# A two-layer scan convolution on one core: output stores over two DMA queues, later statistics, another order in the first sweep

## The chip, the cores and the metric

The kernel runs on one core of a Trainium2 chip. A core has five engines with an instruction stream each: TensorE (PE in the profile) multiplies matrices, VectorE (DVE) and ScalarE (ACT) work on rows of elements, GpSimd (POOL) does so too, and SyncE (SP) only starts transfers. Transfers between the on-chip memory and the DRAM are started by an instruction on SP or on ScalarE, each with a queue of its own (SPq and ACTq in the profile), and are carried out by 16 DMA engines that both queues share. The metric is the device time of one execution in microseconds (us), median of three runs.

## The reference

The input is x with 32 batches, 48 channels, 64 rows and 128 columns, in 32-bit floats. Each of two layers computes `x = x + conv(gn(x))`: gn normalizes each batch over 16 groups of 3 channels, and conv is four recurrent sweeps over the picture, each of the form

```python
def step(w, b):
    def f(carry, inp):
        nxt = inp + _conv1d(carry, w, b)
        return (nxt, nxt)
    return f
...
_, d_rest = jax.lax.scan(step(down_w, down_b), d0, xs[1:])
...
_, u_rest = jax.lax.scan(step(down_w, down_b), u0, seq)
...
_, r_rest = jax.lax.scan(step(right_w, right_b), r0, ws[1:])
...
_, l_rest = jax.lax.scan(step(left_w, left_b), l0, R[Ww - 2::-1])
```

The convolution has 5 taps along the row (or column) and mixes all 48 channels. First the rows are swept downwards and upwards, 63 steps each, then the columns to the right and to the left, 127 steps each. A step needs the one before it, so a sweep is a chain; different batches are independent.

## The kernel before

**Groups and phases.** The 32 batches are cut into four groups of 8. The list `PHASES` fixes an order of twelve phases: eight row phases, each with one layer and one group, sweep down and then up (2 x 63 steps); four column phases, each with one layer and a pair of groups, sweep right and then left (2 x 127 steps). In the profile a sweep has a name such as step_00d: layer, group or pair, direction. Phases are counted from 0 here; phases 2, 6, 10 and 11 are the column phases, and 10 and 11 make the output of the second layer.

**A step.** `step` (L629) issues nine products of 128x128 (L640), which the profile shows as 18 matmuls, into three PSUM tiles; VectorE adds bias and input to each tile and writes the new row or column back in place (L649). The next step's matmuls read that.

**Memory.** The picture of a phase lies in three slots of `arena`; four more pieces, `stage`, hold tiles in passing. Rows and columns need different layouts. The change of layout goes through the DRAM: `move_rows` (L500) stores finished rows or loads rows, in pieces by E8 = 8 rows; `load_unit` (L544) loads one of the six units of a quarter (j = 0 to 3, 32 columns each) for a column phase. A quarter that doesn't fit is spilled and fetched again (`spill_unit`, L559). All transfers are started in one helper, so the profile shows them at L182; without a queue argument they go to SP.

**First group.** Before the first sweep nothing can overlap, so `first_group` (L911) writes out its order by hand. It loads the input in two parts (L945: rows 0 to 31 and 32 to 63, two rows of the picture side by side), takes statistics, permutes each row into the layout of the kernel (`permute`, L473, four copies at L482 per row), stores it (`put_out`), loads it back in the right partitions (`move_rows`), and scales it with the statistics: `scale_rows` (L517) by 24 activations on ScalarE (L525), `scale_at_once` (L529) by two operations on VectorE or GpSimd (L536). The permuted rows of the second part pass through a ring of three places, `more`, in weight tiles that aren't filled yet; row r takes place r mod 3.

**Other groups and the agenda.** Everything beside the sweeps is put on a list, `agenda`, with a due time counted in steps (`at`, L719). Before each step, all entries that have come due are issued (`catch_up`, L1043), and `in_order` (L186) ties every instruction behind the last one of the same engine. So a due time fixes the place of the work in the instruction stream of its engine, and an engine takes its stream in order. `plan_input` (L732) enters the reading of groups 1 to 3: chunks are loaded, permuted on GpSimd and measured by ScalarE (`take_others`, L331: sums at L347, squares at L339). After the last chunk `scaling` (L245) is entered through `spread`, one piece a step: short operations on VectorE, TensorE and ScalarE that turn the sums into scale and offset.

**Seams.** Where a column phase follows directly on the row phase of the same pair (phases 1 and 2, phases 5 and 6), `plan_rows` (L754) stores the last rows in smaller pieces, in `cuts`, and `plan_cols` (L789) loads the first quarter's matching pieces over ScalarE's queue.

**Output of the second layer.** For each unit of phases 10 and 11, in the order of the quarters 3, 2, 1, 0 and in each quarter six units, `load_residual` (L572) loads the layer's input into one of two tiles, over ScalarE's queue (6 or 8 transfers); `add_permuted` (L605) adds it to the result in eight operations on GpSimd (L614), permuting, into one of two tiles; `store_result` (L618) stores it to `out` (12 or 16 transfers, 96, 64 or 32 KB, in runs of 128 bytes), over SP's queue. The unit after next waits for both tiles. On SP's queue the loads of phase 11 stand among these stores. The last quarter of phase 11 goes another way (`last_loads`, `last_results`, L864): its residuals are loaded into free space, VectorE adds (L871), and ScalarE, GpSimd and VectorE share 48 permuting copies (L879) before `store_result`.

Of the kernel before, what the change touches and what calls it, by code (L numbers as in the profile page):

```python
# [35 lines left out]
P = ODD + C  # L36
# [5 lines left out]
GB = 8  # L42
E8 = 8
# [48 lines left out]
def kernel(  # L92
# [8 lines left out]
    nc = tc.nc  # L101
    B, _, H, W = x.shape
# [78 lines left out]
    def dma(dst, src, queue=None):  # L181
        (queue or nc.sync).dma_start(dst, src)  # L182
# [435 lines left out]
    def store_result(k, j, i, perm):  # L618
        pair = PHASES[k][2]
        o, r = divmod(i, 2)  # L620
        both = out[2 * pair * GB : 2 * (pair + 1) * GB]
        dst = both.rearrange("b c (a e) w -> e a c b w", e=E8)[..., j * WQ : (j + 1) * WQ]
        src = perm.rearrange("p (a b n) -> p a b n", a=HH, b=2 * GB)
        for a in range(HH):
            for e, c0, c1, p0 in pieces(o):
                dma(dst[e, r * HH + a, c0:c1], src[p0 : p0 + c1 - c0, a])


    def step(key, weights, b_at, src, inp, dst, whole, part):  # L629
# [89 lines left out]
    def at(t, fn, *args):  # L719
        agenda.append((t, len(agenda), fn, args))  # L720

    def spread(t, gen, every):


        def go(t):
            if next(gen, "end") != "end":
                at(t + every, go, t + every)
                agenda.sort(key=lambda a: a[:2])

        at(t, go, t)  # L730

    def plan_input(g, times, work, lag, nats, perms):  # L732

        stats = InputStats(f"x{g}", GB // 2 if g == 1 else 0)
        rows = nats[0].shape[-1] // W
        ahead, pieces_of = len(nats), rows * W // BN
        per = rows * W * GB // perms[0].shape[-1]
        for j, t in enumerate(times):
            nat = nats[j % ahead]
            if j == 0 and g > 1:  # L740
                at(t - 7, take_in, g, 0, nat)
            for i in range(per):
                perm, r = perms[i % len(perms)], i * rows // per
                at(t + i * work / per, permute, nat, r, perm, [nc.gpsimd])
                at(t + i * work / per + 4, put_out, g, 2 * rows * j + r, perm, rows)
            for b in range(stats.nv):
                at(t + lag + 1.25 * b, stats.take, pieces_of * j, nat, b)
            at(t + lag, stats.take_others, pieces_of * j, nat)
            if j + ahead < len(times):
                free = t + max(work, lag + 1.25 * stats.nv, 7)  # L750
                at(free, take_in, g, 2 * rows * (j + ahead), nat)
        spread(t + work + lag, scaling(f"x{g}", 0, g, stats, x_masks), 1)

    def plan_rows(k, t0, prev):  # L754
        if k == 1:
            ahead, scaled = (-34, -18, 2, 18), (-14, -2, 17, 33)
        elif prev == "cols":
            ahead, scaled = (-28, -12, 4, 20), (-13, 3, 19, 35)
        else:
            ahead, scaled = (-54, -43, 0, 11), (-22, -8, 16, 30)  # L760
        if k:
            for i in range(4):
                at(t0 + ahead[i], move_rows, k, i * LOAD, (i + 1) * LOAD, False)
                at(t0 + scaled[i], scale_rows, k, i * LOAD, (i + 1) * LOAD)

        cuts = list(range(0, H + 1, E8))
        following = PHASES[k + 1][0] == "cols"
        if following and follows(k + 1):
            cuts = [0, E8 // 2] + cuts[1:]
        for h0, h1 in zip(cuts, cuts[1:]):  # L770
            t = t0 + 2 * (H - 1) - h0
            if k == 0:
                t += 24 if h0 >= HALF else 40
            elif not following:
                t = t0 + 92 + 5 * (H - h1) / E8 + (34 if h1 <= HALF else 0)
            at(t, move_rows, k, h0, h1, True)
        at(
            t0 + H - 1,
            nc.gpsimd.tensor_copy,
            last.rearrange("p (o n) -> p o n", o=NG),  # L780
            row(k, H - 1),
        )
# [6 lines left out]
    def plan_cols(k, t0, prev):  # L789
        _, layer, pair = PHASES[k]  # L790
        n = 2 * NG
        after = prev == "cols"
        for i in range(n):
            if follows(k) and UNITS[i][1] == 1:
                other = nc.scalar
                at(t0 - 13 + i, load_unit, k, 0, i, 2, NH, 0, E8, other)
                at(t0 - 6 + i / n, load_unit, k, 0, i, 1, 2, 0, E8, other)
                at(t0 - 3, load_unit, k, 0, i, 0, 1, E8 // 2, E8, other)
                at(t0, load_unit, k, 0, i, 0, 1, 0, E8 // 2, other)
                at(t0 + 1.5, load_unit, k, 1, i)  # L800
            else:
                early = 30 if after else 46 if k == 2 else 70
                at(t0 - early + 2 * i, load_unit, k, 0, i)
                at(t0 + (3 if after else 0.5 if follows(k) else -24 + 2 * i), load_unit, k, 1, i)
            at(t0 + (38 if after else 8) + 2 * i, load_unit, k, 2, i)
            at(t0 + 33 + 2 * i, spill_unit, k, i, False)
            at(t0 + 50 + 2 * i, load_unit, k, 3, i)
        final = k == len(PHASES) - 1
        left = t0 + W - 1
        end = left + W - 1  # L810
        for i in range(n):
            at(left + 64 + 2 * i, spill_unit, k, i, True)
        units = []
        for n_done, j in enumerate((3, 2, 1, 0)):
            every = 4.5
            if j == 0 and PHASES[k + 1 if not final else k][0] == "rows":
                every = 7
            units += [(left + 34 + 32 * n_done + every * i, j, i) for i in range(n)]
        stats = None
        if layer == 0:  # L820
            stats = ResultStatsV(f"r{2 * pair}"), ResultStatsA(f"r{2 * pair + 1}")
        tiles = [stage[:, i] for i in range(4)]
        nats, perms = (tiles, None) if layer == 0 else (tiles[0:2], tiles[2:4])
        ahead = len(nats)

        for u, (t, j, i) in enumerate(units):
            nat = nats[u % ahead]
            o, half = UNITS[i]
            if u < ahead:
                at(left + 16, load_residual, k, j, i, nat)  # L830
            elif not (final and j == 0):
                at(units[u - ahead][0] + (3 if layer == 0 else 5), load_residual, k, j, i, nat)
            if layer == 0:
                at(t, add_residual, k, j, i, nat)
                at(t + 4, keep_result, k, j, i)
                unit = quarter(k, j)[:, half, o]
                if half == 0:
                    for b in range(GB):
                        at(t + 5 + b, stats[0].take, j, o, unit, b)
                else:  # L840
                    at(t + 1, stats[1].take, j, o, unit)
            elif not (final and j == 0):
                perm = perms[u % 2]
                at(t, add_permuted, k, j, i, nat, perm, [nc.gpsimd])
                at(t + 5, store_result, k, j, i, perm)
        if layer == 0:
            t = units[-1][0] + 14
            g = 2 * pair
            spread(t, scaling(f"r{g}", 1, g, stats[0], r_masks), 1)
            spread(t + 20, scaling(f"r{g + 1}", 1, g + 1, stats[1], r_masks), 1)  # L850
        if final:
            at(left + 97, last_loads, k)
            at(end + 4, last_results, k)
# [57 lines left out]
    def first_group():  # L911
# [38 lines left out]
        perms = [spare["down1"][0:P, 0 : W * GB]]  # L950
        perms += [row_views(0)[0][0:P, o, 24:32].rearrange("p h n -> p (h n)") for o in range(NG)]
        more = [spare[k][0:P, 0 : W * GB] for k in ("down1", "right", "left")]

        def permute_row(i, r, *engines):
            permute(parts[i], r, (more if i else perms)[r % (3 if i else 4)], engines)

        def put_row(i, r):
            put_out(0, i * HALF + r, (more if i else perms)[r % (3 if i else 4)], rows)

        def rows_by_product(h0, n):  # L960
            src = parts[0][0:C].rearrange("p b (r k e) -> p e r k b", k=NK, e=E8)
# [50 lines left out]
        for _ in scaling("x0", 0, 0, stats, x_masks):  # L1012
            pass
        scale_at_once(0, 0, 4, nc.vector)
        scale_at_once(0, 4, 8, nc.gpsimd)
        for r in range(2, 8):
            permute_row(0, r, nc.scalar if r % 2 else nc.gpsimd)
            put_row(0, r)
        scale_rows(0, 8, 16)
        for r in range(3):  # L1020
            permute_row(1, r, nc.gpsimd)
            put_row(1, r)
        move_rows(0, 16, 32, False)
        scale_rows(0, 16, 24)
        for r in range(3, 16):
            permute_row(1, r, *([nc.gpsimd] if r < 12 else [nc.gpsimd, nc.scalar]))
            put_row(1, r)
        scale_rows(0, 24, 32)
        move_rows(0, 32, 48, False)
# [77 lines left out]
```

## Time and profile before

| What | us |
|---|---|
| median of three runs (4600.73 to 4604.13) | 4602.15 |
| the profiled execution, first to last instruction | 4604.0 |
| first matmul of step_00d starts | 109.9 |
| last matmul of step_00d starts | 288.8 |
| step_00r (phase 2), first and last matmul start | 712.0, 987.8 |
| step_10l (phase 10), first and last matmul start | 3589.5, 3844.7 |
| step_11r (phase 11), first and last matmul start | 3855.5, 4234.0 |
| step_11l, first and last matmul start | 4234.3, 4489.6 |

The granted clock of TensorE over the span is 0.959. The profile's list of waits names an engine and line, what ended the wait, and three numbers: us in total, how often, and the longest. A wait that needed several things is put down to the one that came last. The chain of waits is followed backwards from the last instruction: each piece is what the next one waited for. The windows give, for each stretch, the busy time of each engine and the share of time in which the 16 DMA engines had a packet in work; the share is a sum over packets and can exceed 1 a little where packets of two queues overlap. Of the stores to `out`, 384 have 96 KB and take 2.6 us from issue to landing (median); the issue of a store itself takes 0.52 us of SP (median).

### The profile page before, as it was taken

What the parts mean: (1) busy time and instruction counts of PE and PEld (TensorE: products, weight loads), DVE (VectorE), ACT (ScalarE), POOL (GpSimd) and SP (SyncE); (2) the same over time, 40 slices, a digit from 0 to 9 for tenths busy, and PEclk for the clock granted to TensorE, in tenths of its full rate; (3) what the DMA queues carried; (4) which work ended last, traced back from release to release, by engine and by line L of the source; (5) the groups of instructions that cost most, each with busy time, mean ns of one, the idle gap of its engine ahead of it and who ended that gap; (6) DMA issues with size and microseconds to landing.
All of it is one profiled execution on the core that took longest, in us unless ns stands there. A gap on an engine that the chain in (4) does not pass through costs nothing.

```text
span 4604.0 us, 90833 instructions
## 1 busy us (share of the span) xinstructions
PE 4169.6 (91%) x36632; PEld 4137.1 (90%) x36632; DVE 2196.7 (48%) x6594; ACT 1185.1 (26%) x2330; POOL 906.7 (20%) x925
## 2 busy tenths in 40 slices
PE   3789998989999999979999999999999996759990
PEld 1789998989999999979999999999999996659990
DVE  5354443446655444434456654444444442324443
ACT  1553301435775435000025944230000000000000
POOL 4342001224322020000024300000000254400544
PEclk9899998999999999989999999999999998879995
DMA  8989789856989989489028989383780288880599
GB/s 164 176 163 155 116 146 180 209 106 208 228 168 158 154 153 154 74 140 209 13 86 240 206 142 154 52 142 74 134 196 1 46 186 166 168 205 1 108 207 162
DMA packets 2124133, 661.56 MB, mean 144 GB/s; under 512 B 2010816, under 2 KB 2063808, under 8 KB 2092224
## 3 DMA queue, kind: packets, MB, share of 16 engines
q1 hardware_dynamic: 2103040, 599.10, 68.2%
q10 hardware_dynamic: 20672, 56.65, 5.0%
q8 instruction: 288, 4.72, 0.5%
q14 instruction: 133, 1.09, 0.1%
HBM read 378.70 MB, written 277.11 MB: 142 GB/s over the span
## 4 chain that ended last, share of the span: by engine, by line
PE 68%; DMA 18%; SPq 4%; ACT 4%; POOL 3%; issue 1%; DVE 1%; ACTq 0%; POOLq 0%; DVEq 0%
PE step_01r L640 6%; PE step_10r L640 6%; PE step_00l L640 6%; PE step_01l L640 6%; SPq L182 4%; DMA arena<-in_x 4%; DMA out<-arena 4%; DMA arena<-mid 3%; PE step_10l L640 3%; PE step_11r L640 3%; PE step_00u L640 3%; PE step_11d L640 3%; PE step_11u L640 3%; PE step_02u L640 3%; PE step_12u L640 3%; PE step_13u L640 3%
## 5 line engine op out<-in xcount | busy, mean ns | idle before, releaser
L525 ACT ACTIVATE arena<-arena,offset,scale 128x256 f32<-128x256 f32 (+1 forms) x816 | 584.7, 812 | 431.4 <-DMA arena<-xin 148.6
L614 POOL TENSOR_TENSOR arena<-arena 128x256 f32<-128x256 f32 x336 | 350.3, 1078 | 987.1 <-DVE arena L649 701.7
L482 POOL COPY arena<-arena 112x256 f32<-112x256 f32 x414 | 244.6, 647 | 759.9 <-DMA arena<-in_x 417.9
L879 ACT COPY arena<-arena 128x256 f32<-128x256 f32 x18 | 10.7, 645 | 1474.8 <-DMA out<-arena 1449.0
L594 POOL TENSOR_TENSOR arena<-arena 128x2048 f32<-128x2048 f32 x48 | 217.7, 4559 | 841.9 <-PE step_01l L640 536.3
L640 PE MATMUL step_11r<-arena,wright 128*128 128x128 f32 x2286 | 267.0, 281 | 122.5 <-DVE arena L649 80.3
L640 PEld LDWEIGHTS step_11r<-arena,wright 128*128 128x128 f32 x2286 | 264.6, 197 | 124.8 <-DVE arena L649 81.9
L416 ACT ACTIVATE junk<-arena 128x256 f32<-128x256 f32 x192 | 129.6, 675 | 718.3 <-DMA arena<-xin 562.1
L640 PE MATMUL step_00r<-arena,wright 128*128 128x128 f32 x2286 | 261.1, 278 | 40.8 <-DMA arena<-upa 25.8
L640 PEld LDWEIGHTS step_00r<-arena,wright 128*128 128x128 f32 x2286 | 260.3, 195 | 41.6 <-issue 25.9
L640 PE MATMUL step_01r<-arena,wright 128*128 128x128 f32 x2286 | 257.8, 276 | 24.0 <-DMA arena<-upa 24.0
L640 PEld LDWEIGHTS step_01r<-arena,wright 128*128 128x128 f32 x2286 | 257.5, 193 | 24.3 <-issue 24.1
L640 PE MATMUL step_00l<-arena,wleft 128*128 128x128 f32 x2286 | 256.2, 275 | 0.0
L640 PE MATMUL step_10r<-arena,wright 128*128 128x128 f32 x2286 | 256.1, 275 | 0.0
L640 PEld LDWEIGHTS step_10r<-arena,wright 128*128 128x128 f32 x2286 | 255.7, 192 | 0.3
L640 PE MATMUL step_11l<-arena,wleft 128*128 128x128 f32 x2286 | 255.7, 275 | 0.0
L640 PEld LDWEIGHTS step_00l<-arena,wleft 128*128 128x128 f32 x2286 | 255.6, 192 | 0.0
L640 PEld LDWEIGHTS step_11l<-arena,wleft 128*128 128x128 f32 x2286 | 255.4, 192 | 0.1
L640 PE MATMUL step_01l<-arena,wleft 128*128 128x128 f32 x2286 | 255.4, 275 | 0.0
L640 PE MATMUL step_10l<-arena,wleft 128*128 128x128 f32 x2286 | 255.4, 275 | 0.0
L640 PEld LDWEIGHTS step_10l<-arena,wleft 128*128 128x128 f32 x2286 | 255.3, 192 | 0.0
L640 PEld LDWEIGHTS step_01l<-arena,wleft 128*128 128x128 f32 x2286 | 255.3, 192 | 0.0
(177 smaller groups left out, 7048.1 us busy)
## 6 DMA issues: line engine op xcount, KB each, us to landing
xin<-arena SPq DMA_DIRECT2D x96, 384.0 KB, 5.4
arena<-xin SPq DMA_DIRECT2D x96, 384.0 KB, 8.4
mid<-arena SPq DMA_DIRECT2D x96, 384.0 KB, 7.8
arena<-mid SPq DMA_DIRECT2D x192, 192.0 KB, 4.3
upb<-arena SPq DMA_DIRECT2D x192, 192.0 KB, 3.9
arena<-mid ACTq DMA_DIRECT2D x192, 192.0 KB, 4.4
arena<-upb SPq DMA_DIRECT2D x96, 384.0 KB, 11.1
out<-arena SPq DMA_DIRECT2D x384, 96.0 KB, 2.6
```

Source lines behind the costliest of these rows:

```text
L182: (queue or nc.sync).dma_start(dst, src)
L416: nc.scalar.activation(junk[:, 0:n], view[:, b], AF.Identity, accum_out=self.sum[:, i, j : j + 1])
L482: copy(dst[:, r, q], src[:, r0 + r, q])
L525: nc.scalar.activation(args[0], args[0], AF.Identity, bias=args[2], scale=args[1])
L594: nc.gpsimd.tensor_tensor(unit, unit, nat, ALU.add)
L614: engines[(2 * a + s) % len(engines)].tensor_tensor(dst[:, a, s], res[:, a, s], inp[:, a, s], ALU.add)
L640: nc.tensor.matmul(part(whole(ps[o]), -s), weights[:, i, FULL * (o - NG * s - i + 1) : FULL * (o - NG * s - i + 2)], part(src(i), s), star ...
L879: copy(dst[:, a, s], src[:, a, s])
```

## The change

Seven edits, in five places.

1. In `store_result` the stores of the first two of a unit's four row blocks stay on SP's queue, those of the last two go to ScalarE's. This holds for phases 10 and 11 and for the last quarter.
2. The residual load of layer 1 is due at 4.9 instead of 5 after the unit whose tile it reuses. That unit's store is due at 5; so on ScalarE's queue the load now comes first.
3. The pieces of `scaling` for group 2 begin 8 steps later, those for group 3 begin 5 steps later.
4. At the two seams the last eight rows are cut into rows 2 to 7 and rows 0 to 1, where they were cut into rows 4 to 7 and rows 0 to 3; the load of the larger piece is due 1.5 steps before the column phase instead of 3.
5. In `first_group` rows 4 to 7 are scaled by ScalarE (`scale_rows`) instead of GpSimd (`scale_at_once`).
6. The copies of rows 3, 5 and 7 of the first part, and half of those of rows 12 to 15 of the second part, move from ScalarE to GpSimd. Four rows of the second part instead of three come before the loading of rows 16 to 31.
7. The ring of the second part has seven places instead of three; the new four lie in slot 2.

```diff
@@ store_result
         for a in range(HH):
             for e, c0, c1, p0 in pieces(o):
-                dma(dst[e, r * HH + a, c0:c1], src[p0 : p0 + c1 - c0, a])
+                to = nc.sync if a < HH // 2 else nc.scalar
+                dma(dst[e, r * HH + a, c0:c1], src[p0 : p0 + c1 - c0, a], to)
@@ plan_input
-        spread(t + work + lag, scaling(f"x{g}", 0, g, stats, x_masks), 1)
+        spread(t + work + lag + (0, 0, 8, 5)[g], scaling(f"x{g}", 0, g, stats, x_masks), 1)
@@ plan_rows
         if following and follows(k + 1):
-            cuts = [0, E8 // 2] + cuts[1:]
+            cuts = [0, E8 // 4] + cuts[1:]
@@ plan_cols
-                at(t0 - 3, load_unit, k, 0, i, 0, 1, E8 // 2, E8, other)
-                at(t0, load_unit, k, 0, i, 0, 1, 0, E8 // 2, other)
+                at(t0 - 1.5, load_unit, k, 0, i, 0, 1, E8 // 4, E8, other)
+                at(t0, load_unit, k, 0, i, 0, 1, 0, E8 // 4, other)
...
-                at(units[u - ahead][0] + (3 if layer == 0 else 5), load_residual, k, j, i, nat)
+                at(units[u - ahead][0] + (3 if layer == 0 else 4.9), load_residual, k, j, i, nat)
@@ first_group
         more = [spare[k][0:P, 0 : W * GB] for k in ("down1", "right", "left")]
+        more += [slot[2][0:P, i * W * GB : (i + 1) * W * GB] for i in range(4)]
...
-            permute(parts[i], r, (more if i else perms)[r % (3 if i else 4)], engines)
+            ring = more if i else perms
+            permute(parts[i], r, ring[r % len(ring)], engines)
...
-            put_out(0, i * HALF + r, (more if i else perms)[r % (3 if i else 4)], rows)
+            ring = more if i else perms
+            put_out(0, i * HALF + r, ring[r % len(ring)], rows)
...
         scale_at_once(0, 0, 4, nc.vector)
-        scale_at_once(0, 4, 8, nc.gpsimd)
+        scale_rows(0, 4, 8)
         for r in range(2, 8):
-            permute_row(0, r, nc.scalar if r % 2 else nc.gpsimd)
+            permute_row(0, r, nc.gpsimd)
             put_row(0, r)
         scale_rows(0, 8, 16)
-        for r in range(3):
+        for r in range(4):
             permute_row(1, r, nc.gpsimd)
             put_row(1, r)
         move_rows(0, 16, 32, False)
         scale_rows(0, 16, 24)
-        for r in range(3, 16):
-            permute_row(1, r, *([nc.gpsimd] if r < 12 else [nc.gpsimd, nc.scalar]))
+        for r in range(4, 16):
+            permute_row(1, r, nc.gpsimd)
             put_row(1, r)
```

## The prediction

> **What bounds the kernel now.** I read first the page's busy times, then the list of what TensorE waited for over the whole run.
>
> ```profile
> PE 4169.6 (91%) x36632; PEld 4137.1 (90%) x36632; DVE 2196.7 (48%) x6594; ACT 1185.1 (26%) x2330; POOL 906.7 (20%) x925
> ...
> q1 hardware_dynamic: 2103040, 599.10, 68.2%
> q10 hardware_dynamic: 20672, 56.65, 5.0%
> ```
>
> TensorE is the spine: 24 sweeps in series, each matmul 275 ns. No edit touches a matmul, so all that can be won is the 9% where it stands still. SP's queue (q1) carries 100 times the packets of ScalarE's (q10).
>
> ```profile
> PE step_11r L640 <- DVE arena L649: 80.3, 6, 22.5
> ...
> PE step_00d L640 <- DVE arena L649: 39.9, 3, 16.6
> PE step_00r L640 <- DMA arena<-upa: 25.8, 1, 25.8
> PE step_11r L640 <- DMA arena<-upb: 24.5, 2, 14.0
> PE step_01r L640 <- DMA arena<-upa: 24.0, 1, 24.0
> PE step_11r L640 <- DMA arena<-mid: 17.6, 1, 17.6
> PE step_00r L640 <- DVE arena L649: 15.0, 2, 12.5
> ```
>
> Columns: total us, times, longest. Five places: phase 11 going right (step_11r: 80.3 + 24.5 + 17.6 = 122.4), the first sweep (39.9 after a start at 109.9), the two seams (25.8 and 24.0), 15.0 in step_00r, and, further down the list, 7.4 in step_10u. Besides them the tail: the last matmul starts at 4489.6, the span ends at 4604.0, 114 us.
>
> What VectorE waited for between 940 and 990, where the 15.0 fall:
>
> ```profile
> DVE mean_x_x L365 <- ACT junk L347: 12.7, 1, 12.7
> DVE neg_x_x L370 <- ACT junk L339: 5.2, 1, 5.2
> ```
>
> VectorE takes its instructions in order, and the statistics of group 2 were put into its stream before ScalarE had the sums; the step's own evictions stood behind them. Step_10u's 7.4 is the same for group 3 (L365 waits 5.2, then L366 takes 3.1).
>
> One cycle of the output of phase 10, from the chain of waits (start, us, what):
>
> ```profile
> 3797.46 2.13 POOL arena L614 x2
> 3799.61 0.31 ACTq L182
> 3799.96 4.45 DMA arena<-mid
> 3804.48 0.32 SPq L182
> ...
> 3809.77 2.19 DMA out<-arena
> 3812.11 2.12 POOL arena L614 x2
> 3814.25 0.31 ACTq L182
> ```
>
> 14.6 us per unit: the last adds of a unit free a residual tile, ScalarE's queue loads it, an SP store waits for that load although it doesn't read it, seven stores are issued (5.3 us), the last lands, and only then POOL has its place for the next adds. The odd link is in the built program: its hardware-queue transfers use eight semaphores in turn, over both queues, so each transfer waits for the one eight before it. POOL needs 8 x 1.08 = 8.6 us for a unit; the cycle, not POOL, sets 14.6.
>
> Then the windows (PE, PEld, DVE, ACT, POOL, clock, DMA share, GB/s):
>
> ```profile
> 3660.00:3835.00 175.00, 175.00 (x1570) 175.00 (x1569) 83.54 (x262) 0.00 (x0) 106.54 (x102) 1.00 0.86 182
> ...
> 4056.00:4106.00 50.00, 3.84 (x18) 3.06 (x18) 1.05 (x3) 0.00 (x0) 0.00 (x0) 0.54 1.02 269
> ...
> 4545.00:4604.00 59.00, 0.00 (x0) 0.00 (x0) 20.96 (x17) 8.88 (x15) 17.20 (x19) 0.50 0.82 135
> ```
>
> While TensorE stands in step_11r the DMA engines are full (1.02, also in 3844 to 3890 and 3954 to 3992). Before those stalls they are not: 0.86. Phase 11's loads come late since the output before them on SP's queue ran late.
>
> **What the Trainium skill says.** "DMA: Bandwidth & Descriptors", section "Issuing engines are not separate DMA queues": a second issuing engine saves only the issue time, since all transfers share 16 DMA engines. The trace agrees for the stalls: at a share of 1.02 a second queue can add nothing. "Perfetto Trace Analysis", section "What "DMA-bound" means", separates full DMA engines from a full issuing sequencer: here the stalls are the first kind, and 4545 to 4604, with SP issuing a store every 0.55 us and the engines at 0.82, the second. "SBUF — State Buffer", section "Who interferes with whom": a VectorE operation with two SBUF inputs and a GpSimd one that reads SBUF exclude each other for a whole instruction. It agrees: at L536 VectorE's multiply took 1.75, its add 4.86 beside POOL's 5.01. "TensorE: Matmul & The Clock Gate", section "What's actually happening": an idle TensorE restarts at half clock. It agrees: step_11r is busy 267.0, the unstalled step_11l 255.7, so 11.3 us for its three stalls.
>
> **The change, part by part.** Sums are against the profiled span, 4604.0; the three timed runs (4600.73 to 4604.13, median 4602.15) are 1.9 lower at the median.
>
> *Statistics 8 and 5 steps later.* A step is 2.01 us (step_10l: 127 in 255.2, 3589.5 to 3844.7). Group 2's wait begins at 963.7, its sums are there at 976.4 and its squares at 983.4; 8 steps later is 979.8, and the second wait is a step behind, 981.8: 15.0 becomes about 1.6. Group 3: 1680.8 + 10.1 = 1690.9, sums at 1686.0, so all 7.4 go. Group 2's coefficients are read over 100 steps later; group 3's 17 steps later (starts[4] + 104 against 87), and there only ScalarE would wait, 22 steps before the rows are due. With 2.7 of half-clock (step_00r is busy 5.4 more than step_11l, over two stalls): **-24**.
>
> *First sweep.* POOL's scaling of rows 4 to 7 goes (5.01 + 4.85), ScalarE gets 24 activations instead; for 128x128 one is 0.51 pipelined, for half of it I estimate 0.45: 11 us, from 103.3 to 114, when row 4 is due. ScalarE loses 12 + 8 copies of 0.65 and their waits (8.5 and 12.3 are the longest), so rows 8 to 15, scaled at 123.9 to 136.2 now, start at 114: the 7.3 gap goes to about 2. POOL takes those 20 (+13), but its 18.3 us wait for a free place, 136.7 to 155.0, shrinks with seven places instead of three; the last row is put out near 164 instead of 177. The 16.6 gap before row 24 (ScalarE held by its late copies) goes. But row 48 waits for transfers, and from 100 to 260 the DMA engines are at 0.94: at most 0.06 x 160 = 9.6 to win. I take **-7** (bounds 0 and -10); the rest reappears as a wait at row 32 or 48.
>
> *Seams.* Rows 2 to 7 now go out together two steps before the end (before: rows 4 to 7, four steps before), and rows 0 and 1 last. The same 20 stores; behind the last step there is half the data but still ten issues; the last reads are 2 transfers instead of 5, at 0.44 each. The later larger part can cost 4 us (two steps), the fewer reads win up to 6 us beside SP's 8 KB loads. I take **-1** each, -2.
>
> *Stores on two queues.* 640 stores, 320 of them moved, behind 320 residual loads on ScalarE's queue; ScalarE computes nothing there before the tail. The 4.9 puts a unit's next residual load ahead of its moved stores; the load waits for the unit's last add, which the stores need anyway, so the stores come at most 8 x 0.45 = 3.6 us of issue later. What it buys: SP has seven stores per unit, not thirteen, and rows 2 and 3 don't stand behind the landing of a load. The cycle then tends to POOL's 8.6 or the DMA engines' own pace. What can be won is DMA idleness: 0.14 x 175 = 24 before the first stall, and between stalls (0.77 of 64, 0.81 of 64) 15 + 12: 51 at most, 0 at least. I take two thirds, **-34**. Tail: 0.09 x 190 = 17 and 0.18 x 59 = 11, 28 at most. ScalarE has 18 copies there, each tile's behind the stores of the tile before (6 to 8 x 0.55), which costs some of it; **-14**.
>
> Sum: 24 + 7 + 2 + 34 + 14 = 81: 4523, or **4521** at the median.
>
> **Rivals.**
>
> *The DMA engines are the limit all the same* (0.22): for it the 1.02 in every stall, against it the 0.86 before. Only statistics and first sweep count: 4604 - 31 - 1.9 = 4571.
>
> *All idleness goes* (0.15): 24 + 10 + 5 + 51 + 28 = 118: 4484. For it POOL's 8.6 against 14.6; against it the two-place buffers.
>
> *Slower: ScalarE's queue becomes the cycle* (0.11). Place: phases 10 and 11, 24 + 18 units. If the eight semaphores put the moved stores behind the landing of the loads and the next loads behind the landing of the stores, a unit takes 2.1 + 3.6 + 4.45 + 8 x 0.55 + 2.2 = 16.8, 2.2 more than 14.6: 42 x 2.2 = 92, less 33 for the other edits: +59, 4661. It decides from 33 / 42 = 0.8 us per unit. Against it: the stores' data wait is already met when the load is issued.
>
> *Nothing* (0.02): the delayed statistics meet later sums, since their loads move too, and the rest cancels: 4602.
>
> **How the numbers follow.** Forecast 0.50, with its own range 4490 to 4550. The overall range 4478 to 4579 takes in nearly all of that, most of the full-DMA case and half of the all-idleness case: 0.5 + 0.2 + 0.1. Under 0.2% (9 us) a measurement can't tell from no change: faster 0.87, same 0.02, slower 0.11.
>
> **What would show it.** No wait over 2 us in step_00r's end and step_10u; ps statistics eight steps into step_00l. Step_00d ending near 282 instead of 289. POOL's cycle in phase 10 at 11 to 12 us, DMA share 3660 to 3835 over 0.92, and step_11r waiting 80 to 95 instead of 122. The last matmul near 4423, with the tail near 100. I am wrong if the cycle stays at 14 or if ScalarE's queue waits for POOL longer than SP's does.

## The result, and the profile after

| | before | after |
|---|---|---|
| median, us (range) | 4601.44 (4597.2 to 4604.13) | 4548.98 (4547.18 to 4553.63) |
| ratio, with its 95% interval | | 0.9888 (0.9871 to 0.9905) |
| profiled execution, us | 4604.0 | 4546.3 |
| first matmul of step_00d / end of step_00d | 109.9 / 289.1 | 106.6 / 279.9 |
| wait at the first / second seam | 25.8 / 24.0 | 29.2 / 29.3 |
| step_00r, first matmul to end | 276.2 | 257.4 |
| step_10u, first matmul to end | 138.6 | 128.55 |
| waits in step_11r, total | 122.4 | 85.7 |
| end of step_11l, the last sweep | 4489.9 | 4422.4 |
| from there to the end | 114.1 | 123.9 |

The kernel became 1.1% faster, 52 us by the medians and 57.7 by the profiled spans. The queues on the page of the kernel after (packets, MB, share of 16 engines):

```profile
q1 hardware_dynamic: 1901312, 573.92, 66.5%
q10 hardware_dynamic: 222400, 81.83, 9.5%
```

ScalarE's queue (q10) has ten times the packets it had; the sum over both queues is unchanged. TensorE does the same 36632 matmuls. What its sweeps waited for in the kernel after (total us, times, longest):

```profile
PE step_11r L641 <- DVE arena L650: 37.6, 4, 18.8
PE step_00d L641 <- DVE arena L650: 34.8, 3, 19.2
PE step_11r L641 <- DMA arena<-mid: 32.8, 2, 16.9
PE step_01r L641 <- DMA arena<-upa: 29.3, 1, 29.3
PE step_00r L641 <- DMA arena<-upa: 29.2, 1, 29.2
PE step_11r L641 <- DMA arena<-upb: 15.3, 1, 15.3
```

The three rows of step_11r add up to 85.7. The row of step_00r for VectorE is gone. The two rows for `upa`, the seams, have grown.

**Did a unit of the output become faster?** The chain of waits of the kernel after, one unit of phase 10 (start, us, what), between two additions on POOL:

```profile
3719.95 1.09 POOL arena L614
...
3722.02 2.98 DMA out<-arena
...
3725.03 0.31 ACTq L182
...
3728.22 5.06 DMA out<-arena
...
3733.37 1.08 POOL arena L614
```

The unit takes 13.4 us. The old order of add, load, store is gone, but in its place two stores land one after the other. What ScalarE's queue issues at 3725.03 is a residual load. It waits for the landing of the store that SP issued at 3722.02, which it doesn't read; the two use the same one of the eight semaphores. From there on six loads and then the first moved stores are issued one by one, and POOL goes on when the store issued at 3728.2 has landed. ScalarE's queue holds in turn the loads of one unit and the stores of the unit two before it, and it runs late: the stores that it issues from 3727.7 on belong to the unit whose last addition ended at 3709.9. In that unit and the next four the moved stores begin to leave 13.7 to 18.6 us after the unit's last addition.

From the end of the first unit of phase 10 to the end of the twelfth, POOL needs 151.0 us; before it was 154.3. So the output itself hardly gained. In 175 us of phase 10, SP issued 150 stores before (3660 to 3835); after (3645 to 3820), SP issued 67 and ScalarE 74. From 185 to 10 us before the end of step_10l it is 150 in both kernels.

**What gained is what stood behind the stores.** The timeline of SP's queue, kernel before (start, duration, what, how many), where phase 10 ends at 3845.0:

```profile
3789.89 45.67 SPq L182 DMA_DIRECT2D out<-arena  x47
3835.67 15.79 SPq L182 DMA_DIRECT2D arena<-upb  x10
```

And of the kernel after, where phase 10 ends at 3814.3:

```profile
3760.15 18.40 SPq L182 DMA_DIRECT2D out<-arena  x12
3779.22 23.23 SPq L182 DMA_DIRECT2D arena<-upb  x10
```

The loads of phase 11 are in the same place of SP's stream as before, but with half the stores ahead of them. Counted from the end of step_10l, the first of the 80 is issued at -35.1 instead of -9.3, the ninth at -16.6 instead of 5.3, the last at 239.5 instead of 277.4: 37.9 earlier, and the waits of step_11r fell by 36.7. By the end of step_10l the stores issued are 160 before and 166 after.

That the split of the stores is the cause is shown by experiment 4. That it works through the place of these loads is read from the timelines; no run moved the loads forward without the split.

The windows (PE, PEld, DVE, ACT, POOL, clock, DMA share, GB/s) between the first and second stall, kernel before:

```profile
3900.00:3920.00 20.00, 20.00 (x182) 20.00 (x181) 9.50 (x31) 0.00 (x0) 10.71 (x11) 1.00 0.77 161
```

And of the kernel after, ahead of the first stall and between the first and second:

```profile
3645.00:3820.00 175.00, 169.79 (x1521) 169.60 (x1519) 81.21 (x254) 0.00 (x0) 93.44 (x90) 1.00 0.95 189
...
3860.00:3880.00 20.00, 20.00 (x181) 20.00 (x181) 9.60 (x30) 0.00 (x0) 15.00 (x15) 1.00 1.13 186
```

The idle time of the DMA engines was used, for loads: from 60 us before the end of step_10l to 240 after it they moved 206 GB/s instead of 178, and 177 without the split (experiment 4). But the share overstates it. Ahead of the first stall it rose from 0.86 to 0.95 and the bytes only from 182 to 189 GB/s; a packet of 128 bytes took 14.0 ns there in the mean instead of 13.0.

**Where the end was lost.** The timeline of ScalarE's queue after the last matmul, kernel after:

```profile
4435.10 13.54 ACTq L182 DMA_DIRECT2D arena<-mid  x17
4448.69 6.90 ACTq L182 DMA_DIRECT2D out<-arena  x6
```

These are the last of 48 residual loads that ScalarE's queue issues from 4409.3 on: 40 of `last_loads`, then the 8 of the 15th of the 18 units. Behind them come the moved stores of the 13th unit, whose tile the 15th waits for. The chain of waits of the kernel after for the same time shows why the loads take so long, one landing after the other:

```profile
4418.69 5.18 DMA arena<-mid
4423.89 6.39 DMA arena<-mid
...
4442.42 6.24 DMA arena<-mid
...
4449.16 6.09 DMA out<-arena
```

POOL stands still meanwhile, in the kernel after for 38.5 us in one piece:

```profile
POOL arena L614 <- DMA out<-arena: 38.5, 1, 38.5
```

Before, the stores were on the other queue. POOL stood still at the same place in that kernel too, for the 15th unit's own residual, but for 31.7 us:

```profile
POOL arena L614 <- DMA arena<-mid: 33.3, 2, 31.7
```

From the end of the first of the 18 units to the end of the last it took 240.9 us before and 262.1 after (+21.2). Of this the longer pause is 6.8. The three units behind it are the larger part: they end 37.5 us after the 15th, where it was 24.4 (+13.1). The last quarter's own stores, from the last addition on POOL to the end, took 58.4 before and 46.4 after (-11.9): together the 9.8 of the table, but for 0.5.

### The profile page after: what moved, and what is told of

The parts are those of the page before. It is cut to its first block, busy times and chain, and to the rows that moved or that the text cites. A ratio compares the mean times of both kernels' runs of the same rounds, so it can differ in the third digit from the quotient of the medians.

```text
span 4546.3 us, 90798 instructions
## 1 busy us (share of the span) xinstructions
PE 4163.2 (92%) x36632; PEld 4132.1 (91%) x36632; DVE 2180.9 (48%) x6594; ACT 1183.5 (26%) x2334; POOL 907.7 (20%) x943
## 4 chain that ended last, share of the span: by engine, by line
PE 77%; DMA 15%; SPq 2%; ACT 2%; POOL 1%; ACTq 1%; issue 1%; DVE 0%; POOLq 0%; DVEq 0%
DMA out<-arena 6%; PE step_01r L641 6%; PE step_00r L641 6%; PE step_10r L641 6%; PE step_00l L641 6%; PE step_01l L641 6%; DMA arena<-mid 4%; PE step_11r L641 3%; PE step_00u L641 3%; PE step_11d L641 3%; PE step_02u L641 3%; PE step_11u L641 3%; PE step_10u L641 3%; PE step_13u L641 3%; PE step_13d L641 3%; PE step_12u L641 3%
## 5 line engine op out<-in xcount | busy, mean ns | idle before, releaser
L525 ACT ACTIVATE arena<-arena,offset,scale 128x256 f32<-128x256 f32 (+2 forms) x840 | 594.7, 802 | 449.3 <-DVE arena L650 151.8
L482 POOL COPY arena<-arena 112x256 f32<-112x256 f32 x458 | 270.9, 648 | 764.1 <-DMA arena<-in_x 469.0
L641 PE MATMUL step_11r<-arena,wright 128*128 128x128 f32 x2286 | 267.3, 281 | 85.7 <-DVE arena L650 37.6
L641 PE MATMUL step_01r<-arena,wright 128*128 128x128 f32 x2286 | 258.8, 277 | 29.3 <-DMA arena<-upa 29.3
L641 PE MATMUL step_00r<-arena,wright 128*128 128x128 f32 x2286 | 257.4, 276 | 29.2 <-DMA arena<-upa 29.2
L641 PE MATMUL step_00l<-arena,wleft 128*128 128x128 f32 x2286 | 256.3, 275 | 0.0
```

The source lines that it names most:

```text
L482: copy(dst[:, r, q], src[:, r0 + r, q])
L525: nc.scalar.activation(args[0], args[0], AF.Identity, bias=args[2], scale=args[1])
L641: nc.tensor.matmul(part(whole(ps[o]), -s), weights[:, i, FULL * (o - NG * s - i + 1) : FULL * (o - NG * s - i + 2)], part(src(i), s), star ...
```

## The experiments

They were run in three groups, each group on one chip beside the kernel before, whose median was 4609.5 in the first (experiments 1 to 4), 4596.7 in the second (5 to 8) and 4607.95 in the third (9 to 12). So times are compared inside a group. One thing must be known for reading single profiles: seven kernels with the same code up to there reached the end of step_10l between 3814.3 and 3831.8, through waits in the row phases and at the seams that vary by some us each. Where a part before phase 10 is judged, it is held against a profile of the same chip.

**1. The seams undone** (x1_seams_back, against the kernel after)

```diff
-            cuts = [0, E8 // 4] + cuts[1:]
+            cuts = [0, E8 // 2] + cuts[1:]
...
-                at(t0 - 1.5, load_unit, k, 0, i, 0, 1, E8 // 4, E8, other)
-                at(t0, load_unit, k, 0, i, 0, 1, 0, E8 // 4, other)
+                at(t0 - 3, load_unit, k, 0, i, 0, 1, E8 // 2, E8, other)
+                at(t0, load_unit, k, 0, i, 0, 1, 0, E8 // 2, other)
```

> The changed kernel with its seams put back: cuts at four rows, the larger piece's load 3 steps ahead. Theory (the larger piece leaves too late and pushes the last rows): the two waits before step_00r and step_01r, 29.2 and 29.3 now, fall to 25.8 and 24.0 as in the kernel before, and the time falls by 8 to 10 us, to about 4540. Rival (the seams are longer because what runs around them has moved, not because of the cuts): both waits stay at 29 and the time at 4549.

Measured: 4548.78 (4547.81 to 4551.56), ratio 0.9874 (0.9855 to 0.9893). TensorE's waits at the seams in this kernel:

```profile
PE step_00r L641 <- DMA arena<-upa: 25.6, 1, 25.6
PE step_01r L641 <- DMA arena<-upa: 24.5, 1, 24.5
```

The waits are the old ones again. So the longer waits came from the new cuts: in the ten profiles with them the two waits are 29.2 to 32.3, in the four with the old cuts 23.0 to 25.8. The total, expected 8 to 10 us lower, can't show it: the ratio is 0.9874 where the kernel after had 0.9888 beside another median, and their intervals overlap. The three other kernels of this group have the new cuts and the same code up to phase 10, and they reached the end of step_10l at 3821.6, 3822.0 and 3825.4, this one at 3814.5: 7 to 11 us earlier.

**2. Phase 11's first three quarters on SP's queue alone** (x3_ph11_sp)

```diff
-                to = nc.sync if a < HH // 2 else nc.scalar
+                to = nc.scalar if a >= HH // 2 and (k < len(PHASES) - 1 or j == 0) else nc.sync
```

> The changed kernel, but in phase 11 the units of quarters 3, 2 and 1 store over SP's queue alone; phase 10 and the last quarter stay divided. Theory (in phase 11 the moved stores stand behind some 46 residual loads on ScalarE's queue, which holds GpSimd up): from the first to the last of the 18 units 241 us instead of 262, the tail after the last matmul about 103 instead of 124, time 4528. Rival (full DMA engines set the tail, whichever queue issues): 262 and 124 stay, time 4549.

Measured: 4550.99 (4545.76 to 4555.44), ratio 0.9877 (0.986 to 0.9894). The 18 units take 242.8 us instead of 262.1, POOL's pause in them is 27.4 instead of 38.5, and the tail after step_11l is 111.8 instead of 123.9. For these 18 units the second queue is a loss. The total of 4528 was missed, though: the end of step_10l comes at 3825.4 instead of 3814.3 and step_11r waits 92.8, so the shorter tail doesn't show in it.

**3. The last quarter's residual loads on SP's queue** (x5_last_loads_sp)

```diff
-    def load_residual(k, j, i, nat):
+    def load_residual(k, j, i, nat, queue=nc.scalar):
...
-                    nc.scalar,
+                    queue,
...
-            load_residual(k, 0, i, nat)
+            load_residual(k, 0, i, nat, nc.sync)
```

> The changed kernel, with the residual loads of the last quarter (40 transfers) issued on SP's queue instead of ScalarE's. Theory (it is these loads in front of the moved stores that lengthen phase 11): GpSimd's pause of 38 us before the last four units shrinks to 25 or less, since half of the stores then get past, time 4535. Rival (the loads only change places, and SP's half of the stores now waits behind them): the pause stays at 35 to 45 and the time at 4549 or above.

Measured: 4544.37 (4542.73 to 4550.47), ratio 0.9866 (0.9849 to 0.9882). The 18 units take 245.5, POOL's pause ahead of the last four is 26.8 instead of 38.5, and the three units after it follow in 8.1, 8.1 and 11.7 us instead of 13.1, 11.8 and 12.6. The tail is 107.3, 16.6 less than in the kernel after; the total fell short of the 4535 expected. That the tail grew by `last_loads` standing ahead of the moved stores is shown by this run and the one before.

**4. No split: all stores on SP's queue again** (x4_no_split)

```diff
-                to = nc.sync if a < HH // 2 else nc.scalar
+                to = nc.sync
...
-                at(units[u - ahead][0] + (3 if layer == 0 else 4.9), load_residual, k, j, i, nat)
+                at(units[u - ahead][0] + (3 if layer == 0 else 5), load_residual, k, j, i, nat)
```

> The changed kernel with all stores back on SP's queue and the residual load due at 5: everything but the division of the stores. Theory: step_11r waits 120 again instead of 86 (+35), the tail after the last matmul is 114 instead of 124 (-10), time 4575. Rival (the division does nothing, and phase 11 gained because the phases before it left more room): step_11r waits about 86 and the time is 4540 to 4550.

Measured: 4586.12 (4582.88 to 4590.26), ratio 0.9954 (0.9939 to 0.9969). Step_11r waits 123.9. SP's queue in this kernel, where phase 10 ends at 3821.6:

```profile
3770.36 42.62 SPq L182 DMA_DIRECT2D out<-arena  x46
3813.09 17.29 SPq L182 DMA_DIRECT2D arena<-upb  x10
```

Its loads of phase 11 leave at -8.5 from the end of step_10l, the last at 279.1, as in the kernel before. Against experiment 2, whose tail is the nearest (111.8 against 117.2), the split of phase 10's and the last quarter's stores is worth 35 us in the total. What the residual load's 4.9 instead of 5 does by itself was not tried: whether the moved stores would gain by standing ahead of the loads stays open.

**5. The statistics at their old places** (x2_stats_back)

```diff
-        spread(t + work + lag + (0, 0, 8, 5)[g], scaling(f"x{g}", 0, g, stats, x_masks), 1)
+        spread(t + work + lag, scaling(f"x{g}", 0, g, stats, x_masks), 1)
```

> The kernel after, with the statistics of groups 2 and 3 at their old places. Theory (their waits stood on the path, and nothing later takes the gain back): step_00r gets its 15.0 us of waiting for VectorE back and step_10u its 7.4, with slow restarts 28.9 us in all: 4578 (4570 to 4583). Rival (the DMA engines work on during such a wait, so that the later stalls shrink by part of it): the two waits come back, but the waits at row 48 of step_02d or those of step_11r get shorter, and the total is 4563 or less.

Measured: 4559.45 (4556.3 to 4569.84), ratio 0.9919 (0.9901 to 0.9937). Both numbers missed. TensorE's waits in this kernel:

```profile
PE step_00r L641 <- DVE arena L650: 5.6, 2, 4.0
...
PE step_10u L641 <- DVE arena L650: 1.9, 2, 1.7
```

The waits come back, but with 5.6 and 1.9 instead of 15.0 and 7.4. Experiment 7, with the same code up to phase 10 but for this edit and on the same chip, has step_00r at 257.3 and step_10u at 128.55; here they take 266.1 and 131.1. In all eleven profiles with the edit they take 257.3 to 258.7 and 128.6. So in this profile the edit is worth 11.3 in these two sweeps, where the profile of before promised 28.9. Later waits did not take the difference: step_11r waits 83.3. The reason lies ahead of it: the sums and squares of group 2 are complete 261.1 us after the first matmul of step_00r, in the kernel before 271.4.

**6. The first group undone** (x6_first_back)

```diff
-        more += [slot[2][0:P, i * W * GB : (i + 1) * W * GB] for i in range(4)]
...
-        scale_rows(0, 4, 8)
+        scale_at_once(0, 4, 8, nc.gpsimd)
...
-            permute_row(0, r, nc.gpsimd)
+            permute_row(0, r, nc.scalar if r % 2 else nc.gpsimd)
...
-        for r in range(4):
+        for r in range(3):
...
-        for r in range(4, 16):
-            permute_row(1, r, nc.gpsimd)
+        for r in range(3, 16):
+            permute_row(1, r, *([nc.gpsimd] if r < 12 else [nc.gpsimd, nc.scalar]))
```

> The kernel after, with the first group's edits undone (ring of three places, GpSimd scales rows 4 to 7, ScalarE makes its share of the permuted copies). Theory (the 9.2 us by which step_00d ended earlier come from these edits and are kept to the end): step_00d ends at 287 to 290, the waits of step_00d are about 40, the total is 4558 (4554 to 4563). Rival (the transfers of groups 1 and 2 set rows 16, 32 and 48 of later sweeps, which take the gain back as they took that of the seams): the total is 4546 to 4552.

Measured: 4561.18 (4548.79 to 4565.68), ratio 0.9915 (0.9897 to 0.9933). Step_00d ends at 286.5, in experiment 7 at 279.1, and step_01d at 559.1 against 550.1; the end of step_10l is 3827.25 against 3818.0, so the 9 us are kept. This doesn't hang on two profiles: in the ten with these edits step_01d ends at 549.9 to 554.5, in the four without them at 559.1 to 562.5.

**7. Half the bytes, the same transfers** (x7_half_bytes)

```diff
-                dma(dst[e, r * HH + a, c0:c1], src[p0 : p0 + c1 - c0, a], to)
+                dma(dst[e, r * HH + a, c0:c1, 0:GB], src[p0 : p0 + c1 - c0, a, 0:GB], to)
```

> The kernel after, with each store of the output cut to the first 8 of its 16 batches: as many transfers, on the same queues, behind the same waits, with half the packets and bytes; half of the output is not written. Theory (after the split the 16 DMA engines set the pace of a unit, their share being 0.95): half of the 0.44 that the stores took is gone, a unit of phase 10 falls from 13 to 10 us or less, and step_11r waits 45 us or less instead of 86; total about 4480 to 4505 with a tail of 90 to 105. Rival (the chain of landings through the eight semaphores sets the pace, and fuller DMA engines only accompany it): a unit stays at 12 us or more, the DMA share between 3645 and 3820 falls to about 0.73, step_11r waits 70 or more, total 4525 or more.

Measured: 4488.4 (4482.28 to 4495.84), ratio 0.976 (0.9739 to 0.978), with half of the output unwritten. The result lies between the two expectations: from the end of the first unit of phase 10 to that of the twelfth it takes 138.1 instead of 151.0, step_11r waits 60.0, the tail is 82.8. The window of this kernel:

```profile
3645.00:3820.00 175.00, 173.89 (x1558) 173.70 (x1556) 82.89 (x259) 0.00 (x0) 106.17 (x103) 1.00 0.84 180
```

With half of the stores' bytes gone the share falls from 0.95 only to 0.84, since phase 11's loads leave earlier (the first 50.7 us before the end of step_10l instead of 35.1) and fill in; and a unit still needs 11 to 13 us, more than POOL's 8.6. Bytes are part of it, not all.

**8. Seams undone and the last loads on SP** (z1_both): the edits of experiments 1 and 3 together.

> The kernel after, with the seams undone and the last quarter's residual loads on SP's queue. Theory (the seams' longer waits are taken back before phase 10, the last loads are worth some 5 us in the tail): seam waits about 25 each, tail 107, total 4544 (4539 to 4549). Rival (the two add up): 4537 or less.

Measured: 4521.87 (4521.28 to 4527.56), ratio 0.9834 (0.9815 to 0.9854): the fastest that writes the whole output, its interval clear of that of the kernel after (0.9871 to 0.9905). It waits 25.2 and 23.0 at the seams. Against the 31.6 and 30.1 of experiment 7 that is 6.4 and 7.1 less, and the end of step_10l comes at 3806.4 instead of 3818.0. With a tail of 109.8 instead of 123.9 the two add up, as the rival had it.

**9. The kernel after once more** (a0_after_again)

> The kernel after itself, unchanged, as a measure beside the other three: 4545 to 4555 if the time holds from run to run; waits at the seams of about 29 each, step_11r waiting 80 to 95, 118 to 126 from the last matmul to the end.

Measured: 4562.55 (4557.51 to 4567.65), ratio 0.9906 (0.9891 to 0.9922). On this chip it is 13.6 slower than in the first comparison; the kernel before is 6.5 slower. Seam waits of 31.2 and 30.3, 90.3 in step_11r, 124.0 from step_11l to the end: the same places.

**10. The statistics alone** (y2_stats_alone, against the kernel before)

```diff
-        spread(t + work + lag, scaling(f"x{g}", 0, g, stats, x_masks), 1)
+        spread(t + work + lag + (0, 0, 8, 5)[g], scaling(f"x{g}", 0, g, stats, x_masks), 1)
```

> The kernel before with one edit alone: the statistics of groups 2 and 3 come 8 and 5 steps later. Theory (the edit removes whatever of these waits stands, and with the old seams all 28.9 us of it stand): 26 to 30 us less than the kernel before, no wait over 2 us at the end of step_00r. Rival (the edit is worth the 11 us that its removal from the kernel after cost, wherever it stands): 9 to 14 us less.

Measured: 4585.78 (4582.15 to 4597.31), ratio 0.9958 (0.9945 to 0.9972): 22 us less, 13 to 25 by the interval. In the trace step_00r takes 257.7 instead of 276.2 and step_10u 128.55 instead of 138.6, together 28.5, and no wait of them is left; step_01d and step_02d are 3.7 longer. So the total gained a little less than the 26 to 30 expected. In these two sweeps the edit is worth 28.5 alone and 11.3 in the kernel after (experiment 5).

**11. The seams alone** (y3_seams_alone, against the kernel before)

```diff
-            cuts = [0, E8 // 2] + cuts[1:]
+            cuts = [0, E8 // 4] + cuts[1:]
...
-                at(t0 - 3, load_unit, k, 0, i, 0, 1, E8 // 2, E8, other)
-                at(t0, load_unit, k, 0, i, 0, 1, 0, E8 // 2, other)
+                at(t0 - 1.5, load_unit, k, 0, i, 0, 1, E8 // 4, E8, other)
+                at(t0, load_unit, k, 0, i, 0, 1, 0, E8 // 4, other)
```

> The kernel before with one edit alone: the seams cut into rows 2 to 7 and rows 0 to 1. Theory (the seam waits grow by 3 to 5 us each, but the input of group 2 then arrives 7 to 8 us earlier as counted in steps, so that the statistics' waits in step_00r fall from 15 to some 6): seam waits of 29 to 30, step_00r taking 266 to 268 instead of 276 without its seam, and a total 10 us less to 2 us more than the kernel before. Rival (nothing is given back): step_00r keeps 15 us of waits and the total is 7 to 10 us more than the kernel before.

Measured: 4612.69 (4595.58 to 4622.39), ratio 1.0006 (0.9993 to 1.0018): no difference, 5 us more by the medians and between the two expectations. TensorE's waits in this kernel:

```profile
PE step_01r L640 <- DMA arena<-upa: 32.3, 1, 32.3
PE step_00r L640 <- DMA arena<-upa: 29.4, 1, 29.4
...
PE step_00r L640 <- DVE arena L649: 1.3, 1, 1.3
```

The seams wait 11.9 longer than before, and of the 15.0 that step_00r waited for VectorE 1.3 are left: it takes 260.2 instead of 276.2. The sums and squares of group 2 are there 257.1 us after its first matmul instead of 271.4. Only 3.6 of these 14.3 us are the later start of the sweep; for the rest, group 2 is read earlier, and why was not tried. In nine of the ten profiles with the new seams this time is 256.3 to 263.1, in one (experiment 9) 270.9; in the four with the old seams it is 266.3 to 271.4. So the two edits take away the same wait, the seams by bringing the sums forward in the sweep and the statistics by their later place, but the seams not in every execution. Step_10u is the same as before (138.1), so the smaller wait there in experiment 5 doesn't come from the seams; its cause stays open.

**12. The same bytes in twice the transfers** (x8_twice, against the kernel after)

```diff
-                dma(dst[e, r * HH + a, c0:c1], src[p0 : p0 + c1 - c0, a], to)
+                for b in (0, GB):
+                    dma(dst[e, r * HH + a, c0:c1, b : b + GB], src[p0 : p0 + c1 - c0, a, b : b + GB], to)
```

> The kernel after, with each store of the output issued as two, one for each 8 of its 16 batches: the same bytes and packets in twice as many transfers over the same two queues. Theory (after the split a unit's pace is made up about half by the bytes and half by landings waited for one after the other through the eight semaphores, since half the bytes took it from 13.3 to 11.4): a unit of phase 10 takes 15 us or more, step_11r waits 105 or more instead of 86, total 4590 or more. Rival (bytes alone; the 11.4 was the pace of the residual loads): a unit takes 14 us or less, step_11r waits 80 to 95, total 4560 or less.

Measured: 4685.81 (4680.57 to 4688.54), ratio 1.0169 (1.0155 to 1.0183), 123 us more than experiment 9. Step_11r waits 153.3 (90.3 there), the first twelve units take 187.9 (153.5), the 18 units of phase 11 309.3 (262.2), the tail 180.8 (124.0). The window of this kernel:

```profile
3645.00:3820.00 175.00, 175.00 (x1569) 175.00 (x1568) 83.77 (x262) 0.00 (x0) 85.56 (x83) 1.00 0.77 156
```

The DMA engines have the same packets to move and move fewer of them: 0.77 and 156 GB/s, with 0.95 and 187 GB/s in experiment 9. Nor are the queues full of issuing: in these 175 us the issues take 68.6 us of SP's time and 81.2 of ScalarE's. What is left, by elimination, is the waiting of transfers for landings of earlier ones: the traces show eight semaphores for the transfers of both queues, used 423 or 424 times each in the kernel after. No run changed their number. With the 13 us that half the bytes took from twelve units, both count. The reading that fits is that a unit waits for several landings in a row, each of them longer with more bytes in flight.

## Why the prediction was right, and where it was not

The time lay in the range, 28 us above the forecast. Term by term, against the profiled span:

| step | forecast | traces of before and after |
|---|---|---|
| statistics (step_00r after its seam, step_10u) | -24 | -28.9 |
| first sweep (end of step_00d) | -7 | -9.2 |
| seams, with step_01r | -2 | +9.7 |
| waits of step_11r | -34 | -36.7 |
| tail after the last sweep | -14 | +9.8 |
| the rest (step_02d 2.4 shorter) | 0 | -2.4 |
| sum | -81 | -57.7 |

**Statistics.** Right by the traces: no wait is left in step_00r's end or step_10u, and all 22.4 of them went, where 1.6 had been left standing; the matmuls around them became faster by 6.5, where 2.7 were reckoned. But the term can't be taken by itself. Experiments 5, 10 and 11 show that 28.5 holds only with the old seams; with the new ones some 11 were left for it to win in experiment 5's profile.

**First sweep.** Right in size and mechanism. ScalarE's half activations, estimated at 0.45, took 0.40 (24 in 9.6 us, from 103.2 to 112.8). The wait at row 8 (7.3) went, POOL's wait for a place fell from 18.3 to 7.8, and what was not won reappeared at rows 16 (10.4), 32 (5.1) and 48 (19.2, before 15.9). That the gain is kept is shown by experiment 6.

**Seams.** Wrong in sign. "The later larger part can cost 4 us (two steps), the fewer reads win up to 6": the second half failed. The waits grew by 3.4 and 5.3. In the trace of the first seam the last two reads are issued 19.1 and 19.4 us after the start of the last matmul, before the last five from 18.7 to 20.5. But by then four loads of the second quarter have gone out on SP's queue, and six by 20.0, instead of three; the two reads take 7.8 and 9.9 us to land, the five took 5.5 to 6.3. That is read from the trace; the runs show only that the cuts are the cause. The step missed, too, that this wait and that of the statistics are tied: with the new seams group 2's sums come earlier in step_00r, so the sum of edits priced one by one counted waiting there that the seams take away anyway.

**Stores on two queues.** The size was right, -36.7 for -34, and so were its first signs: a DMA share of 0.95 (over 0.92 was said), 85.7 of waits (80 to 95), a last matmul at 4422 (4423). The step that failed is "The cycle then tends to POOL's 8.6 or the DMA engines' own pace", with the 11 to 12 us expected: it stayed at 13 to 14, the sign that I had named for being wrong. Under it lies "the stores come at most 8 x 0.45 = 3.6 us of issue later": in phase 10 they began to leave 13.7 to 18.6 us after the last addition. The loads ahead of them wait for landings of SP's stores, since the link through eight semaphores, which the rival used, spans both queues; a second queue doesn't loosen it. "SP has seven stores per unit, not thirteen" was the part that held, not for the stores but for the loads behind them. So the closeness of -36.7 to -34 is partly luck. Idle DMA time was used, as the sum had it, but not by a faster output, and the two thirds taken of it had no measurement behind them. The sum itself used 0.77 and 0.81 between the stalls, shares of shorter stretches; over the whole of each they are 0.79 and 0.83, so 48 could be won and not 51.

The Trainium skill's sentence in "DMA: Bandwidth & Descriptors", section "Issuing engines are not separate DMA queues", that a second issuing engine saves only the sequencer's time for starting transfers, isn't the whole of it here: the split also changed the order, and phase 11's loads left 26 us earlier against the end of step_10l.

**Tail.** Wrong in sign, +9.8 for -14. The share of the last stores is as forecast, more than used up (58.4 us became 46.4). What was left out is the other work on the queue to which the stores are moved: the prediction placed the moved stores behind a unit's own loads, at most 8, and said nothing of the 40 that `last_loads` puts there at once, ahead of the last four units. Experiments 2 and 3 show it; 16.6 us come back when these loads go by SP's queue.

**The rivals.** Full DMA engines as the only limit is refuted by experiment 4 (35 us for the split) and by experiment 12, whose engines are emptier and whose time is longer. All idleness going is refuted by the 13 us cycle. ScalarE's queue as the cycle came true in its place but not in its size: in phase 10 the chain runs through ScalarE's loads and stores as it said, but with 13.4 us for a unit and not 16.8; only in phase 11 was it slower than before, by 21 us of the 92 that it had for all 42 units.

## What to carry to other kernels

Before work is moved to another queue, list everything that the queue will have ahead of it at each time, also the burst that comes once; and ask what stands behind the work on the queue that it leaves, since that may be what gains. Two edits that remove waits on the same chain are not added: after the first, price the second again. Where transfers wait for landings, count transfers before bytes.

## What the runs showed that was not expected

- Splitting each store in two, at the same bytes, cost 123 us of 4563, while leaving out half of the bytes gained some 60 of 4549 (by the ratios, 0.976 against 0.9888).
- With both queues storing, the DMA share goes over 1: up to 1.15 between the stalls, and 1.11 from 4420 to 4525 in experiment 8, at 171 GB/s; the store-only end of the kernel before had 0.82 at 135 GB/s. In the kernel after, a 128-byte packet takes 13.6 ns in the mean on SP's and 14.3 on ScalarE's queue ahead of the first stall, and 15.0 and 14.6 from 4493 to the end. In the first stall the share went from 1.02 to 1.12 and the bytes only from 180 to 185 GB/s, so there the prediction's reading of full engines holds.
- A kernel with unchanged code up to phase 10 reached its end 17.5 us earlier or later from one profile to another, nearly all of it in the waits of the row phases and at the seams.
